# Mixture-of-experts layer on one core: expert rows gathered in 32-column strips and turned by VectorE instead of TensorE

## The chip, the cores and the metric

The kernel runs on one core of a Trainium2 chip. The metric is the device time of one execution in microseconds (us). Three executions of the kernel before took 930.4, 930.9 and 931.77 us; the median is 930.9 us. Engines are called by these names: TensorE (PE in the profile, with its weight loads as PEld), VectorE (DVE), ScalarE (ACT), GpSimd (POOL), SyncE (SP). An engine name with a q (SPq, ACTq) is that engine's instruction queue, from which DMAs are issued.

## The reference

Everything is float32. `x` has 4 batches of 1024 tokens with 512 columns. Each batch picks one of 64 weight matrices by `itok`; after that linear layer the 4096 tokens go to 8 experts, top-1, with at most 512 tokens per expert:

```python
xf   = x @ W[itok] + b[itok]                   # 4096 x 512
prob = softmax(xf @ Wr);  e = argmax(prob)     # 8 experts
keep = rank of the token within its expert < 512
xe   = xf[dispatch]                            # (8, 512, 512): gathered rows
h    = relu(xe @ W1[e])                        # 512 x 2048 per expert
ye   = (h @ W2[e]) * prob of the token         # 512 x 512 per expert
y[dispatch] += ye
out  = x + y
```

## The kernel before, in words

All large products use Strassen-Winograd steps: a product of 2 x 2 blocks is made of seven products numbered k = 1 to 7, and VectorE makes the sums of blocks that they need. Partial results of several k are accumulated in one PSUM bank (`BANK`, L145: k = 1, 4, 6, 7 in bank x; 3, 5 in y; 2 in z), and between two products of one bank a VectorE or ScalarE instruction reads what has been accumulated so far. A product that follows in the same bank has to wait for that read.

**Stage 1 (0 to 147 us): the batch's linear layer and the router.** Chunks of 512 tokens of `x` are loaded (`load_x`, L245, on SP's queue; the first chunk in four pieces), turned by TensorE (`transpose_x`, L265), multiplied (`linear`, L470), and VectorE adds the bias while it empties PSUM (`plus_bias`, L501, and `finish`, L516). `done` (L509) writes each 256-token result to DRAM, in two arrays `xc0_dram` and `xc1_dram`, one for each half of the columns (1 KB per token and array). The router ranks the tokens and scatters, per expert slot, the token's number and probability into `slots` in DRAM (`rank`, L441). `table` (L637) reads them back, and GpSimd makes row indices of them (L642).

**Stage 2 (147 us to the end): the experts, one after the other, about 96 us each.** `fetch(e)` (L698) is called after the second group of the first layer. GpSimd gathers by indirect DMA (`gather`, L682) the residual rows of `x` for expert e, four gathers of 128 rows x 2 KB, and the rows of the next expert e+1 from `xc0_dram` and `xc1_dram`, eight gathers of 128 rows x 1 KB. `transpose_rows` (L707) turns a tile of 128 rows with four TensorE transposes into PSUM; ScalarE copies them to `xe` (VectorE does it for expert 0), and after the last tile VectorE makes four sums of `xe` blocks (L727 to L733). `xe` has a single buffer, so nothing of the next expert can be written before the last first-layer product of this expert has read it.

The first layer is `first_layer` (L740) for four groups g of hidden units, `xe` as the moving side and W1 as the weights. The second layer (`second_layer`, L795) does the products k = 1, 6, 7 whole, and k = 2, 5, 3, 4 by a second Strassen step: `inner_sums` (L815) makes twelve VectorE sums or differences at most per k, and `inner_product(e, k, q)` (L851) the small products q = 1 to 7, written "(k, q)" below. The order at the end of an expert (L952 to L984) is: second layer 1; inner sums 2; second layer 6; inner sums 5; **turn tile 0 of the next expert**; small products (2,1), (2,5), (2,2), (2,6), (2,3), (2,7); **turn tiles 1 and 2**; (2,4); inner sums 3; second layer 7; inner sums 4; (5,5), (5,2); **turn tile 3**; then the rest of (5,q), (3,q), (4,q). Products (2,7) and (2,4) both write bank x. At the last expert no tiles are turned, since there is no next one. GpSimd scatters the finished rows at the end (L889).

**What sets the order.** The program lists the order of TensorE and of SP's queue by hand (`manual_schedule`). For VectorE, ScalarE and GpSimd the order is worked out when the kernel is built, from the program's order as priority and an expected time at which each instruction's inputs are ready; `soon` and `high_priority` move a call up, `behind` ties it to an earlier instruction. On the chip each engine then runs its list strictly in that order: an instruction whose input is not there holds up everything behind it.

Of the kernel before, what the change touches and what calls it, by code (L numbers as in the profile page):

```python
# [16 lines left out]
P = 128  # L17
# [5 lines left out]
def kernel(  # L23
# [29 lines left out]
    W1G = 3  # L53
    NS = E * SC
    Q = 32
    ROW = 2
# [26 lines left out]
    def unordered(group, ins):  # L83
# [12 lines left out]
    nc.vector.memset(wr_sb, 0.0)  # L96
    nc.scalar.dma_start(
        out=wr_sb[:, :, 0:E], in_=wr.rearrange("(kc p) e -> p kc e", p=P)
    )
    zeros = const.tile([P, T * ROW // P], F32, name="zeros")  # L100
    nc.vector.memset(zeros, 0.0)
    slots = dram.tile([T, ROW], F32, name="slots")
    nc.scalar.dma_start(out=slots.rearrange("(p s) r -> p (s r)", p=P), in_=zeros)
    before = const.tile([P, P], F32, name="before")
# [25 lines left out]


    xc_dram = [dram.tile([T, HD], F32, name=f"xc{j}_dram") for j in range(2)]

    table = const.tile([P, SC, E, ROW], F32, name="table")
    src_row = const.tile([P, NS], I32, name="src_row")
    dst_row = const.tile([P, NS], I32, name="dst_row")

# [36 lines left out]
    def load_w1(e, g):  # L174

        t = w1p.tile([P, 7, HK, HB * P], F32, tag="w1", name=f"w1_{e}_{g}")
        for half in range(2):
            f = half * F // 2 + g * HB * P
            nc.sync.dma_start(
                out=t[:, 2 * half : 2 * half + 2, :, :].rearrange("p a k f -> p (a k) f"),  # L180
                in_=w1[e, :, f : f + HB * P].rearrange("(k p) f -> p k f", p=P),
            )
        w1s[e, g] = t

# [4 lines left out]
    with (  # L189
# [54 lines left out]

        def load_x(c):  # L245
            t = xin.tile([P, XT, D], F32, tag="x", name=f"x_{c}")
            n = 1 if c == 0 else XT
            for j in range(0, XT, n):
                nc.sync.dma_start(
                    out=t[:, j : j + n, :],  # L250
                    in_=xf[c * CT + j * P : c * CT + (j + n) * P, :].rearrange(
                        "(j p) d -> p j d", p=P
                    ),
                )
            xrows[c] = t
# [214 lines left out]
        def linear(b, g, k):  # L470
# [15 lines left out]
            for j in range(2):  # L486
                for kc in range(HK):
# [11 lines left out]
                    )  # L499

            def plus_bias(into, half):  # L501
                return nc.vector.tensor_tensor(
                    into,
                    ps,
                    bias[:, half * HD : (half + 1) * HD].unsqueeze(1).to_broadcast([P, 2, HD]),
                    ALU.add,
                )

            def done(t, i, j):  # L509
                at = c * CT + i * HT  # L510
                nc.sync.dma_start(
                    out=xc_dram[j][at : at + HT, :].rearrange("(j p) d -> p j d", p=P),
                    in_=t,
                )

            def finish():  # L516
# [10 lines left out]
                if k in (2, 3):  # L527
                    t = banks.pop((key, 1 if k == 2 else 6))
                    latest[0] = nc.vector.tensor_tensor(t, ps, t, ALU.add)
                    done(t, 0, int(k == 3))  # L530
                if k == (7 if b < B - 1 else 5):
                    t = banks.pop((key, 7))
                    nc.vector.tensor_tensor(t, banks[key, "y"], t, ALU.add)
                    done(t, 1, 1)
                    if b == LATE:
                        t = banks[key, 6]
                        nc.vector.tensor_tensor(t, banks[key, "y"], t, ALU.add)
                if k == 4:
# [82 lines left out]
        with tc.manual_schedule(engines={mybir.EngineType.PE, mybir.EngineType.SP}):  # L621
            load_x(0)
            load_batch(0)
            load_x(1)
            load_batch(1)
            load_x(2)
            load_batch(2)
            keep_warm(ps_t, 3)
            for i in range(XT):
                transpose_x(0, i)  # L630
            for b in range(B):
                for i, product in enumerate(ORDERS[b]):
                    linear(*(b, *product)[-3:])
                    for f, *at in loads.get((b, i), []) + beside.get((b, i), []):
                        f(*at)
# [21 lines left out]

    rows, residual, xes, hs = {}, {}, {}, {}

    def load_w2(e, when=None):  # L660
# [21 lines left out]
    def gather(e, pool, sources, into, at):  # L682

        n = D // len(sources)
        for j, source in enumerate(sources):
            for c in range(SC):
# [9 lines left out]
                )  # L696

    def fetch(e):  # L698

        at = rowp.tile([P, 2 * SC], I32, tag="at", name=f"at_{e}")  # L700
        n = min(2 * SC, NS - e * SC)
        nc.vector.tensor_copy(at[:, 0:n], src_row[:, e * SC : e * SC + n])  # L702
        gather(e, xr, [xf], residual, at[:, 0:SC])
        if e + 1 < E:
            gather(e + 1, xg, xc_dram, rows, at[:, SC : 2 * SC])

    def transpose_rows(e, c, parts=range(2)):  # L707

        if e not in xes:
            xes[e] = xep.tile([P, 7, HK, HC * P], F32, tag="xe", name=f"xe_{e}")  # L710

        t = xes[e]
        r = rows[e * SC + c]
        half, at = divmod(c, HC)
        n = len(parts)
        lo = parts[0] * HK
        ps = ps_e.tile([P, KC, P], F32, tag="t", name=f"ps_e_{e}_{c}_{lo}")
        for kc in range(n * HK):
            nc.tensor.transpose(ps[:, kc, :], r[:, (lo + kc) * P : (lo + kc + 1) * P], ident)
        (nc.vector.tensor_copy if e == 0 else nc.scalar.copy)(  # L720
            t[
                :, 2 * half + parts[0] : 2 * half + parts[0] + n, :, at * P : (at + 1) * P
            ].rearrange("p b k n -> p (b k) n"),
            ps[:, 0 : n * HK, :],
        )
        if c == SC - 1:
            b11, b21, b12, b22, t1, t2, t4 = (t[:, k, :, :] for k in range(7))  # L727
            if 0 in parts:
                nc.vector.tensor_tensor(t1, b12, b11, ALU.subtract)
            if 1 in parts:  # L730
                nc.vector.tensor_tensor(t2, b22, t1, ALU.subtract)
                nc.vector.tensor_tensor(b12, b22, b12, ALU.subtract)
                nc.vector.tensor_tensor(t4, b21, t2, ALU.subtract)  # L733

# [187 lines left out]
    with tc.manual_schedule(engines={mybir.EngineType.PE, mybir.EngineType.SP}):  # L922
        gather(0, xg, xc_dram, rows, src_row)

        for part, half, then in (
            ([0], 0, [(0, 1)]),
            ([0], 1, [(1, 1), (0, 5), (1, 5)]),
            ([1], 0, [(0, 2)]),
            ([1], 1, [(1, 2)]),
        ):  # L930
# [6 lines left out]
        for e in range(E):  # L937
# [25 lines left out]

            def ahead(*tiles):
                for c in tiles:
                    if e + 1 < E:
                        transpose_rows(e + 1, c)

            second_layer(e, 6)
            inner_sums(e, 5)  # L970
            ahead(0)
            small(*[(2, q) for q in (1, 5, 2, 6, 3, 7)])
            ahead(1, 2)
            small((2, 4))
# [3 lines left out]
            small((5, 5), (5, 2))  # L978
            ahead(3)
            small(  # L980
# [37 lines left out]
```

## Time and profile before

| What | Value |
|---|---|
| Median of three runs | 930.9 us |
| The profiled execution | 930.86 us |
| Span of its instructions (first to last) | 929.1 us |
| TensorE busy in the span, matmuls | 915.9 us |
| TensorE transposes of gathered rows (L719) | 128, of which 112 are of experts 1 to 7 |
| VectorE busy | 654.9 us |
| GpSimd busy | 181.7 us |
| Mean DMA rate | 133 GB/s |
| Granted TensorE clock | 0.998 |
| Packets under 512 B | 8516 of 95727 |

The span is 1.8 us shorter than the time of the same execution; that remainder lies around the instructions. A timeline row gives the start and the length of a group of like instructions, then engine, line, operation, output and inputs, sizes and count, and in brackets how long the engine had been idle before it and what ended that. Matmuls overlap, so a row of eight 128 x 128 products that starts every 0.89 us is listed as 1.06 us long; what counts is the distance from one start to the next. The same holds for VectorE, where a sum of 128 x 512 elements is listed as 0.68 us long and starts every 0.60 us.

### The profile page before, as it was taken

What the parts mean: (1) busy time and instruction counts of PE and PEld (TensorE: products, weight loads), DVE (VectorE), ACT (ScalarE), POOL (GpSimd) and SP (SyncE); (2) the same over time, 40 slices, a digit from 0 to 9 for tenths busy, and PEclk for the clock granted to TensorE, in tenths of its full rate; (3) what the DMA queues carried; (4) which work ended last, traced back from release to release, by engine and by line L of the source; (5) the groups of instructions that cost most, each with busy time, mean ns of one, the idle gap of its engine ahead of it and who ended that gap; (6) DMA issues with size and microseconds to landing.
All of it is one profiled execution on the core that took longest, in us unless ns stands there. A gap on an engine that the chain in (4) does not pass through costs nothing.

```text
span 929.1 us, 13272 instructions
## 1 busy us (share of the span) xinstructions
PE 915.9 (99%) x5318; PEld 817.5 (88%) x5318; DVE 654.9 (70%) x1222; ACT 193.5 (21%) x350; POOL 181.7 (20%) x173
## 2 busy tenths in 40 slices
PE   9999999999999999999999999999999999999996
PEld 6788787889988998899889988999889988998886
DVE  4656684589549954987488847883789368945793
ACT  3323200321132103210331023112311132113200
POOL 0043443060141013201230024001500150012001
PEclk9999999999999999999999999999999999999999
DMA  8475223992372118310841085106520562044001
GB/s 299 157 242 167 81 80 117 343 379 90 100 254 100 46 61 266 127 47 21 275 152 46 1 277 164 58 1 227 182 91 2 202 202 90 2 154 159 1 1 46
DMA packets 95727, 123.32 MB, mean 133 GB/s; under 512 B 8516, under 2 KB 83268, under 8 KB 95474
## 3 DMA queue, kind: packets, MB, share of 16 engines
q1 hardware_dynamic: 85634, 97.54, 31.5%
q0 software_dynamic: 9216, 24.85, 8.1%
q8 instruction: 42, 0.69, 0.3%
q10 hardware_dynamic: 816, 0.08, 0.1%
q14 instruction: 19, 0.16, 0.1%
HBM read 105.96 MB, written 25.23 MB: 141 GB/s over the span
## 4 chain that ended last, share of the span: by engine, by line
PE 64%; issue 18%; DVE 13%; POOL 3%; DMA 1%; ACT 0%; POOLq 0%; DVEq 0%
PE hx L746 19%; PE hy L746 9%; PE yx L856 7%; PE xcx_lin L488 6%; PE hz L746 5%; PE yx L803 4%; PE yy L856 3%; DVE rows L791 2%; PE xcy_lin L488 2%; POOL rows L691 2%; DVE h L160 2%; DVE h L161 2%; PE ps_xT L273 1%; PE xcz_lin L488 1%; DVE h L163 1%
## 5 line engine op out<-in xcount | busy, mean ns | idle before, releaser
L746 PE MATMUL hx<-xe,w 128*128 128x256 f32 x1024 | 237.7, 379 | 1.2 <-DVE xe L720 1.0
L746 PEld LDWEIGHTS hx<-xe,w 128*128 128x128 f32 x1024 | 193.8, 190 | 27.7 <-DVE xe L720 1.2
L889 POOL DMA_INDIRECT out_dram<-rows,dst_row x32 | 32.0, 999 | 465.3 <-DVE rows L791 428.6
L746 PE MATMUL hy<-xe,w 128*128 128x256 f32 x512 | 120.6, 379 | 0.0
L803 PE MATMUL yx<-w_b,h 128*128 128x256 f32 x512 | 113.1, 379 | 0.0
L746 PEld LDWEIGHTS hy<-xe,w 128*128 128x128 f32 x512 | 97.3, 190 | 13.2
L803 PEld LDWEIGHTS yx<-w_b,h 128*128 128x128 f32 x512 | 96.7, 190 | 12.8
L761 ACT COPY s<-hx 128x512 f32<-128x512 f32 x96 | 55.8, 582 | 222.7 <-PE hx L746 222.7
L765 DVE TENSOR_TENSOR h<-hy,s 128x512 f32<-128x512 f32 x64 | 44.1, 688 | 76.0 <-PE hy L746 51.7
L766 ACT ACTIVATE h<-h 128x512 f32<-128x512 f32 x96 | 60.5, 630 | 150.7 <-DVE h L765 150.7
L856 PE MATMUL yx<-w_b,h 128*128 128x128 f32 x640 | 83.4, 275 | 0.7 <-DVE rows L791 0.6
L791 DVE SCALAR_TENSOR_TENSOR rows<-yx,table,rows 128x128 f32<-128x128 f32 (+1 forms) x160 | 59.9, 398 | 30.8 <-PE yx L856 30.7
L856 PEld LDWEIGHTS yx<-w_b,h 128*128 128x128 f32 x640 | 77.3, 192 | 1.1 <-DVE rows L791 1.0
L691 POOL DMA_INDIRECT rows<-in_x_dram,at x32 | 45.2, 1412 | 145.4 <-DVE at L702 106.2
L691 POOL DMA_INDIRECT rows<-xc_dram,at x56 | 58.4, 1043 | 21.4 <-issue 14.3
L746 PE MATMUL hz<-xe,w 128*128 128x256 f32 x256 | 60.6, 379 | 0.6 <-DVE xe L720 0.6
L765 DVE TENSOR_TENSOR h<-hz,s 128x512 f32<-128x512 f32 x32 | 22.0, 688 | 55.4 <-PE hz L746 55.4
L803 PE MATMUL yx<-w_t,h 128*128 128x256 f32 x256 | 56.6, 379 | 0.0
L460 POOL DMA_INDIRECT slots<-row,dest x32 | 36.3, 1136 | 96.4 <-DVE dest L456 87.9
L746 PEld LDWEIGHTS hz<-xe,w 128*128 128x128 f32 x256 | 48.5, 190 | 7.4 <-DVE xe L720 0.9
L803 PEld LDWEIGHTS yx<-w_t,h 128*128 128x128 f32 x256 | 48.6, 190 | 6.6
L856 PE MATMUL yx<-w_t,h 128*128 128x128 f32 x384 | 52.1, 279 | 0.4
(160 smaller groups left out, 1244.3 us busy)
## 6 DMA issues: line engine op xcount, KB each, us to landing
w<-in_L_ffn_W_dram SPq DMA_DIRECT2D x64, 512.0 KB, 4.3
w_b<-in_L_ffn_W_dram SPq DMA_DIRECT2D x32, 1024.0 KB, 10.9
x<-in_x_dram SPq DMA_DIRECT2D x7, 1024.0 KB, 8.7
xc_dram<-s SPq DMA_DIRECT2D x22, 256.0 KB, 2.7
out_dram<-in_x_dram SPq DMA_DIRECT2D x2, 2816.0 KB, 20.3
cw<-in_L_cond_W_dram SPq DMA_DIRECT2D x3, 1024.0 KB, 10.6
out_dram<-in_x_dram SPq DMA_DIRECT2D x1, 2560.0 KB, 12.2
xc_dram<-xc SPq DMA_DIRECT2D x8, 256.0 KB, 2.3
```

The costliest lines, as they stand in the source:

```text
L160: eng.tensor_tensor(s1, a21, a22, ALU.add)
L460: nc.gpsimd.indirect_dma_start(out=slots, out_offset=bass.IndirectOffsetOnAxis(ap=dest[:, j : j + 1], axis=0), in_=row[:, j, :], in_offset ...
L488: nc.tensor.matmul(ps[:, j, :], lhsT=left[:, kc, j * P : (j + 1) * P], rhs=right[k][:, kc, :], start=((k in OPENS or (b, k) == (LATE, 3)) ...
L691: nc.gpsimd.indirect_dma_start(out=into[e * SC + c][:, j * n : (j + 1) * n], out_offset=None, in_=source, in_offset=bass.IndirectOffsetOnA ...
L746: nc.tensor.matmul(ps[:, j, :], lhsT=w1s[e, g][:, LEFT[k], kc, j * P : (j + 1) * P], rhs=xes[e][:, RIGHT1[k], kc, :], start=(k in OPENS an ...
L761: nc.scalar.copy(banks[key, k], ps)
L765: latest[0] = nc.vector.tensor_tensor(into, ps, part, ALU.add)
L766: nc.scalar.activation(into, into, AF.Relu)
L791: nc.vector.scalar_tensor_tensor(row, ps, table[:, half * HC + at, e, 0:1], row, ALU.mult, ALU.add)
L803: nc.tensor.matmul(ps[:, at, :], lhsT=hs[e][:, m // HB, LEFT[k], m % HB, at * P : (at + 1) * P], rhs=w2s[e][RIGHT2[k]][:, m, :], start=(k ...
L856: nc.tensor.matmul(ps, lhsT=left[:, g, :], rhs=right[:, g, :], start=(q in OPENS and g == 0), stop=(q == LAST[BANK[q]] and g == NG - 1), s ...
L889: nc.gpsimd.indirect_dma_start(out=of, out_offset=bass.IndirectOffsetOnAxis(ap=dst_row[:, n : n + 1], axis=0), in_=residual.pop(n), in_off ...
```

## The change

For experts 1 to 7 the rows are no longer gathered whole. The column order of `xc0_dram` and `xc1_dram` is permuted, so that the 256 columns of a half lie in four strips of 64. A gather then fetches, for 32 rows, all four strips, each into its own 32 partitions: 128 descriptors of 256 B. An expert needs 32 such gathers in place of 8. In SBUF the tile is then a set of 32 x 32 squares each of which only has to be turned in place, and four VectorE instructions of 128 x 512 elements per expert (`turn_strips`) do so, writing straight to `xe`. Sixteen TensorE transposes and four ScalarE copies per expert go away. Expert 0 keeps the old way; since the columns of its rows are now permuted, its W1 is loaded in a matching order, by 16 DMAs of 64 KB per group in place of 2 of 512 KB. New index tables (`strips`, `src_strip`) are made once, by four DMAs on ScalarE's queue and eight small GpSimd instructions. Apart from that the first chunk of `x` is loaded through ScalarE's queue, ahead of `wr` and the zeros for `slots`, and one of three warming matmul pairs at the start is dropped.

```diff
@@ load_w1
+            into = t[:, 2 * half : 2 * half + 2, :, :]
+            if e > 0:
...
+                continue
+            rows_of = w1[e, :, f : f + HB * P].rearrange(
+                "(a k q b c) f -> b k c a q f", a=2, k=HK, b=2, c=V
+            )
+            for b in range(2):
+                for k in range(HK):
+                    lo = (b * HK + k) * V
+                    for a in range(2):
+                        nc.sync.dma_start(out=into[lo : lo + V, a], in_=rows_of[b, k, :, a])
@@ linear: plus_bias, done, finish
+            def strip(t):
+                return t.rearrange("p j d -> p (j d)").rearrange(
+                    "p (b j k c) -> p j k b c", b=VB, j=2, c=V
+                )
+            def bank_of(t):
+                return t.rearrange("p j (k b c) -> p j k b c", b=VB, c=V)
...
+                return nc.vector.tensor_tensor(strip(into), bank_of(ps), bank_of(added), ALU.add)
...
-                    out=xc_dram[j][at : at + HT, :].rearrange("(j p) d -> p j d", p=P),
-                    in_=t,
+                    out=xc_dram[j][at : at + HT, :].rearrange(
+                        "(j p) (b d) -> p b j d", p=P, b=VB
+                    ),
+                    in_=t.rearrange("p j d -> p (j d)").rearrange(
+                        "p (b j d) -> p b j d", b=VB, j=2
+                    ),
@@ start
-            load_x(0)
+            load_x(0, nc.scalar)
             load_batch(0)
+            nc.scalar.dma_start(
+                out=wr_sb[:, :, 0:E], in_=wr.rearrange("(kc p) e -> p kc e", p=P)
+            )
+            nc.scalar.dma_start(out=slots.rearrange("(p s) r -> p (s r)", p=P), in_=zeros)
...
-            keep_warm(ps_t, 3)
+            keep_warm(ps_t, 2)
@@ new functions
+    def strip_rows():
+        for b in range(VB):
+            nc.scalar.dma_start(
+                out=strips[b * V : (b + 1) * V].rearrange("r a c e w -> r a (c e w)"),
+                in_=slots.rearrange("(a r s) w -> r a (s w)", a=VB, r=V),
+            )
+        into = src_strip.rearrange("p e (c a) -> p e c a", a=VB)
+        for a in range(VB):
+            row = strips[:, a, :, :, 1].rearrange("p c e -> p e c")
+            nc.gpsimd.tensor_scalar(row, row, FAR, float(T - 1), ALU.add, ALU.min)
+            nc.gpsimd.tensor_scalar(
+                into[:, :, :, a], row, float(VB), strip_at, ALU.mult, ALU.add
+            )
+    def gather_strips(e, at):
+        for half in range(2):
+            for j in range(2):
+                t = xg.tile([P, D], F32, tag="rows", name=f"strips_{e}_{half}_{j}")
+                n = D // (HC * VB)
+                for q in range(HC * VB):
+                    c = half * HC * VB + q
+                    nc.gpsimd.indirect_dma_start(
+                        out=t[:, q * n : (q + 1) * n],
+                        out_offset=None,
+                        in_=xc_dram[j].rearrange("t (b d) -> (t b) d", b=VB),
+                        in_offset=bass.IndirectOffsetOnAxis(ap=at[:, c : c + 1], axis=0),
+                    )
+                rows[e, half, j] = t
+    def turn_strips(e, half, j):
+        t = rows.pop((e, half, j)).rearrange("p (q k c) -> p k q c", k=HK, c=V)
+        into = xe_of(e)[:, 2 * half + j, :, :].rearrange("p k (q r) -> p k q r", r=V)
+        nc.vector.transpose(into, t)
@@ order at the end of an expert
             second_layer(e, 6)
             inner_sums(e, 5)
-            ahead(0)
             small(*[(2, q) for q in (1, 5, 2, 6, 3, 7)])
-            ahead(1, 2)
+            if e + 1 < E:
+                for half in range(2):
+                    for j in range(2):
+                        turn_strips(e + 1, half, j)
             small((2, 4))
             inner_sums(e, 3)
             second_layer(e, 7)
             inner_sums(e, 4)
             small((5, 5), (5, 2))
-            ahead(3)
+            if e + 1 < E:
+                sum_xe(e + 1)
```

## The prediction, made before the changed kernel was run

> **What bounds the kernel now.** First the page: which engine is full, and what the transposes cost as a group (line, engine, operation, output and input, sizes, count, busy us and mean ns, idle time before).
>
> ```profile
> PE 915.9 (99%) x5318; PEld 817.5 (88%) x5318; DVE 654.9 (70%) x1222; ACT 193.5 (21%) x350; POOL 181.7 (20%) x173
> ...
> L719 PE MATMUL ps_e<-ident,rows 128*128 128x128 f32 x128 | 18.3, 273 | 0.4 <-DMA rows<-xc_dram,at 0.4
> L720 ACT COPY xe<-ps_e 128x512 f32<-128x512 f32 x28 | 15.7, 588 | 80.2 <-PE ps_e L719 80.2
> ```
>
> (The second and third line are from the groups by form.) TensorE has no gaps worth naming, at a clock of 0.998, so an instruction less on it is the only thing that shortens the run, provided TensorE then doesn't wait. Hence the second view: who is just behind it at the end of an expert. The windows give span, then busy time of PE, PEld, DVE, ACT, POOL:
>
> ```profile
> 333.10:429.30 96.20, 96.15 (x561) 87.62 (x562) 70.87 (x125) 19.85 (x36) 17.43 (x16) 1.00 0.37 121
> ...
> 401.50:425.20 23.70, 23.70 (x162) 22.18 (x160) 23.63 (x46) 2.78 (x6) 0.00 (x0) 1.00 0.12 42
> ```
>
> Over a whole expert VectorE has 25 us free, but in the stage from which the transposes are taken it is as full as TensorE: 23.63 of 23.70 us. The third view is TensorE's timeline there, for expert 2 (with transposes), then for expert 7, which has no next expert and so no transposes:
>
> ```profile
> 411.70 1.06 PE L856 MATMUL yx<-w_b,h 128*128 128x128 f32 x8
> 412.60 1.04 PE L719 MATMUL ps_e<-ident,rows 128*128 128x128 f32 x8
> 413.47 1.06 PE L856 MATMUL yx<-w_b,h 128*128 128x128 f32 x8
> ```
>
> ```profile
> 892.91 1.16 PE L856 MATMUL yx<-w_b,h 128*128 128x128 f32 x8
> 894.63 1.16 PE L856 MATMUL yx<-w_b,h 128*128 128x128 f32 x8 [0.56 <-DVE rows L791]
> ```
>
> The yx rows are (2,7) and (2,4), of one bank. In expert 2 eight transposes fill the 0.87 us between them; in expert 7, without them, TensorE stands until VectorE has read the bank, and (2,4) starts 1.72 us after (2,7) instead of the usual 0.89: a stall of 0.83. Last, GpSimd's gathers at expert 0:
>
> ```profile
> 203.19 1.45 POOL L691 DMA_INDIRECT rows<-xc_dram,at  x1 [0.30 <-issue]
> 204.94 1.08 POOL L691 DMA_INDIRECT rows<-xc_dram,at  x1 [0.30 <-issue]
> 210.65 1.19 POOL L691 DMA_INDIRECT rows<-xc_dram,at  x1 [4.62 <-DMA rows<-in_x_dram,at]
> ```
>
> They come late and behind a DMA backlog (DMA share about 1.0 from 162 to 212 us).
>
> **1. Transposes off TensorE.** Four take 0.44 us from start to start (406.80 to 407.24), so 16 take 1.75, and seven experts 12.3 us. That is the ceiling. But they were also fillers. Expert 7 shows the same list without them: from the end of second layer 6 (888.20) to the last pair (919.51) is 31.31 us; expert 2 takes 406.80 to 439.09, 32.29. So 0.98 us per expert, not 1.75; the rest is the stall at (2,4). Expert 7 also lacks the xe sums on VectorE. Expert 2 has with them waits of about 0.2 us before (5,6) (425.49) and 0.1 before (5,4), which expert 7 lacks; those stay. I take 0.98 - 0.30 = 0.68, seven times: **-4.8 us**. At expert 0 the wait of 0.4 for a gathered tile in mid-transpose goes too: **-0.4**. ScalarE's 28 copies were beside other work: 0.
>
> **2. Four turns per expert on VectorE.** No turn is in the trace. The nearest row is a 128x512 sum, 0.68 us, 0.60 from start to start: four are 2.4 us. Here the Trainium skill speaks against the change ("VectorE: DVE Perf Modes", section "The three transpose paths" and the rules after it): a 128x128 bf16 takes 311 ns on VectorE, in 32x32 squares, and TensorE is advised where PSUM will do. An expert has 16 such blocks, so by the page 5.0 us (an estimate from its bf16 figure). With either, VectorE's list gets longer where it is full. Inner sums 4 end at 425.2; with 2.4 us ahead of them 427.6, with 5.0 us 430.2. TensorE needs them for (4,5) at 431.05, less the 0.7 gained: 430.3. With the row's figure there are 2.7 us to spare, with the page's 0.1. Inner sums 3 (end 418.8, needed by (3,5) at 426.49) have more. So 0, with the row's figure; with the page's the small PSUM reads also come late, 0 to 1 us per expert. A gain is excluded: nothing leaves VectorE's list.
>
> **3. Gathers: 32 for 8.** A gather is 0.95 us plus 0.30 between, for 1 KB rows and other sizes of piece alike (1.14 mean for the 8-byte scatters). So 1.25 x 32 = 40 us where it was 10. In expert 2 they start at 368.38, end at 408.4, and land (median 3.0) at 411.4. The turns stand in the list after inner sums 5, which end at 413.7; the fourth turn starts at 415.5. The GpSimd scatters behind them come only at 437. So 0, with 2 to 4 us of cover; lost cover stops VectorE, one for one. In bytes nothing changes, but packets are 256 B. "DMA: Bandwidth & Descriptors", section "Specifications", puts the line rate at 512 B and above. The software queue's 24.85 MB take 8.1% of 16 engines' 929 us, so an expert's 1.05 MB take some 3.2 us of all 16 engines (an estimate), twice that if halved in rate, beside a DMA share of 0.37: 0. No run here shows such packets.
>
> **4. The same at expert 0.** Gathers start at 198.1; six are out by 206.0, the queue waits until 210.65, eight are out by 213.2, the other 24 take 30 us: 243.2, landed at about 246. Quarters arrive near 216, 226, 236, 246. The old transposes were at 214 to 231. The first product of expert 1 that needs all four quarters is k = 6, at 248.41 + 3.45 - 1.1 = 250.8; turn and sums need some 2 us after 246. So it just fits **if** VectorE's list has the third and fourth turn behind the other work. If they stand at their place in the program (221 us), VectorE stops, and with it the reads that free TensorE's banks. The list isn't in program order: W1 sums run between the earlier-listed h sums at 361 to 365 us, because readiness counts. So an expected late landing puts the turns later. But the expectation can be early: at 12.18 VectorE waits 0.6 us for a bias DMA placed ahead of ready work. Bounds 0 and about 18 us: (3,5) at 234.0 would wait for a turn at 246.2 and then inner sums 3, 8 x 0.60. I take 0, with doubt.
>
> **5. Between the stages.** xc writes have 1024 runs of 256 B for 256 of 1 KB. One issue was 0.36 us; w_b loads of 1024 runs took 1.41 (5.64 for four). So SP is held about 1 us more per write. Only the last writes count: gathers of the second half start at 151.21, rows are needed at 156.29, and with 1.25 per gather and 3.0 to land the second tile arrives at about 155.5. A delay of 1 to 3 us leaves 0 to 2: **+1.0**. The eight index instructions (0.32 to 0.36 each, 2.8 in all) fit GpSimd's 5.4 us gap before 151.21; in front of the gathers they'd cost up to 2.8. W1 of expert 0: 14 more SP issues per group at 0.36, 5 us, in front of xc writes (88.78) and, at 174, of output copies; two buffers per partial result cover it: 0, at most 2. VectorE's evictions into runs of 32: a permuted read (L368, 287 ns) costs what a plain one does (L81, 286): 0; doubled they'd still fit, 91 of 147 us busy plus 38.
>
> **6. The start.** One warming pair less is 2 x 0.855 = 1.71 us; transposes begin right behind it (6.74). The x pieces, issued 1.14 to 2.95, land 3.5 later, 4.6 to 6.5, so not all can be used; from ScalarE's queue they start no later, and weights (3.99) leave SP up to 1 us earlier. ScalarE's first copy is at 7.82, wr needed at 16: hidden. Bounds 0 and -1.71: **-1.0**.
>
> Sum: -4.8 - 0.4 + 1.0 - 1.0 = -5.2. The profiled execution took 930.86 us (span 929.1 plus 1.8 around it), equal to the median 930.9: about 925.5.
>
> **The rivals.**
> - *A full gain*: VectorE's reads come at once, nothing stalls: 930.9 - 12.3 - 1.7 = 917. Against it stands expert 7's (2,4). Chance 0.05.
> - *Expert 0 stops VectorE* (slower): part 4 by the list of turns in program order, or with turns three and four at the expected, too early, times. A stop of 5 to 18 us, likeliest 12: 925.5 + 12 = 937.5. It decides from 5 us on, that is when a turn stands more than 5 us ahead of its landing. For it: the backlog, the in-order list. Against: readiness is weighed, and 2 us of the list are enough slack once it is. Chance 0.28.
> - *VectorE becomes the bound of every expert*: turns at 5.0 us or more, stalls of 0.7 to 1.5 us seven times: 930 to 936. Chance 0.12.
> - *The forecast*: 920 to 929, chance 0.55.
>
> **How the numbers follow.** A measurement of this kernel tells 0.2% (1.9 us) from no change. Faster: 0.52 of the forecast's 0.55 and the full gain's 0.05, so 0.57; same 0.11, from the edges of all; slower 0.32, from the other two. The range 918 to 940 leaves out the full gain and the worst of the stop.
>
> **What would show it.** (2,4) starting about 1.7 us after (2,7) in experts 0 to 6 (right), or 0.9 (full gain). Experts about 95.5 us apart instead of 96.24. Turns near 0.7 us. In the waits, no VectorE wait for gathered rows; if there is one of many us at expert 0, part 4 failed; if one in each expert, part 3. An end of stage 1 later than now beyond 1 us would show part 5 wrong; a first product (9.44) at about 8.4, part 6 right.

## The result, and the profile after

The changed kernel takes 1000.2 us (median of four runs, 999.16 to 1000.93) where the kernel before takes 930.9: 1.074 times as long, interval 1.072 to 1.076. The forecast was 925.5 with a range up to 940. The profiled execution took 999.16 us with a span of 997.4, 68.3 more than the 929.1 of before.

The experiments ran in seven sessions, and five of these (1, 3, 4, 6 and 7) were disturbed: the kernel before took 931.8 to 932.9 us there instead of 930.8, some of the semaphore updates are missing from every trace, and kernels with many small gathers saw some releases 7 us and more late, so that numbers are compared only within a session.

The page of the changed kernel: engines, the gathers, products that TensorE stood in front of, and the turns (busy us, mean ns, idle before).

```profile
PE 924.4 (93%) x5204; PEld 820.7 (82%) x5204; DVE 670.4 (67%) x1257; ACT 177.9 (18%) x322; POOL 366.5 (37%) x353
...
L753 POOL DMA_INDIRECT strips<-xc_dram,at x224 | 242.0, 1080 | 74.1 <-issue 66.1
...
L929 PE MATMUL yx<-w_b,h 128*128 128x128 f32 x640 | 92.5, 294 | 27.8 <-DVE rows L864 27.7
...
L791 DVE STREAM_TRANSPOSE xe<-strips 128x512 f32<-128x512 f32 x28 | 19.1, 699 | 69.9 <-DMA strips<-xc_dram,at 38.2
```

TensorE has 114 instructions less and is busy for longer, 924.4 us for 915.9: part of its work ran at a lower clock. The 28 turns take 0.70 us each, and VectorE stood for 69.9 us in front of them. The waits of the changed kernel say for what (us in total, times, longest):

```profile
DVE xe L791 <- DMA strips<-xc_dram,at: 38.2, 8, 8.6
DVE xe L791 <- issue: 31.7, 7, 7.1
PE yx L929 <- DVE rows L864: 27.7, 16, 5.2
PE yx L876 <- DVE h L163: 24.0, 7, 6.5
```

These are 15 waits, about two for each of the seven experts that are turned so. All are for gathered strips, those named "issue" too: each of the 15 turns starts 0.27 to 0.28 us after the landing of the last gather of its own tile. TensorE's waits are for the VectorE work that is queued behind the turns. In expert 2 VectorE's timeline shows the order of its list:

```profile
428.14 0.69 DVE L838 TENSOR_TENSOR h<-hy,s 128x512 f32<-128x512 f32 x1 [0.61 <-PE hy L819]
428.75 1.29 DVE L791 STREAM_TRANSPOSE xe<-strips 128x512 f32<-128x512 f32 x2
429.97 0.70 DVE L162 TENSOR_TENSOR h<-h 128x512 f32<-128x512 f32 x1
434.96 0.71 DVE L791 STREAM_TRANSPOSE xe<-strips 128x512 f32<-128x512 f32 x1 [4.28 <-DMA strips<-xc_dram,at]
435.60 0.65 DVE L163 TENSOR_TENSOR h<-h 128x512 f32<-128x512 f32 x1
436.16 0.75 DVE L164 TENSOR_TENSOR h<-h 128x512 f32<-128x512 f32 x1
436.84 0.68 DVE L165 TENSOR_TENSOR h<-h 128x512 f32<-128x512 f32 x1
437.44 0.72 DVE L162 TENSOR_TENSOR h<-h 128x512 f32<-128x512 f32 x1
442.74 0.71 DVE L791 STREAM_TRANSPOSE xe<-strips 128x512 f32<-128x512 f32 x1 [4.57 <-issue]
```

The first turns stand right behind the last first-layer sum (L838), and not behind inner sums 5. The third stands among the sums of `h` of the last group (the first L162 to L165), the fourth among those of inner sums 2 (the second L162 on). Both are reached before their strips are there; GpSimd's last gather for this expert is

```profile
439.94 0.94 POOL L753 DMA_INDIRECT strips<-xc_dram,at  x1 [0.30 <-issue]
```

TensorE in the same stretch:

```profile
436.30 1.99 PE L876 MATMUL yx<-w_t,h 128*128 128x256 f32 x8 [3.01 <-DVE h L163]
438.13 1.05 PE L929 MATMUL yx<-w_b,h 128*128 128x128 f32 x8
439.02 1.06 PE L929 MATMUL yy<-w_b,h 128*128 128x128 f32 x8
439.91 1.06 PE L929 MATMUL yz<-w_b,h 128*128 128x128 f32 x8
445.72 2.07 PE L929 MATMUL yx<-w_b,h 128*128 128x128 f32 x8 [4.75 <-DVE rows L864]
447.59 1.92 PE L929 MATMUL yy<-w_b,h 128*128 128x128 f32 x8
449.29 1.91 PE L929 MATMUL yx<-w_b,h 128*128 128x128 f32 x8
451.65 1.27 PE L929 MATMUL yx<-w_b,h 128*128 128x128 f32 x8 [0.44 <-DVE rows L864]
```

Two stops, 3.01 and 4.75 us, and behind the second the products start 1.7 to 1.9 us apart, not 0.89. The windows show why (span, busy time of PE, PEld, DVE, ACT, POOL, then the granted clock):

```profile
370.90:476.68 105.78, 97.57 (x547) 88.47 (x545) 73.22 (x130) 17.59 (x32) 44.14 (x41) 0.97 0.35 110
440.80:445.70 4.90, 0.17 (x2) 0.00 (x0) 2.96 (x7) 0.00 (x0) 0.08 (x1) 0.94 0.04 8
445.70:452.70 7.00, 6.54 (x32) 6.24 (x33) 5.54 (x12) 0.00 (x0) 0.00 (x0) 0.56 0.00 0
452.70:459.70 7.00, 7.00 (x35) 6.17 (x35) 6.84 (x13) 0.00 (x0) 0.00 (x0) 1.00 0.00 0
```

For the 7 us behind the stop the clock is 0.56. Every stop of 4.6 us or more in this trace brings a clock of 0.5, and of the eight stops of 2.4 to 3.6 us half do. Which ones, the trace shows too. Its nine drops of the clock up to the last product all begin on one grid of 3.413 us: the first is at 216.39 us, and the others (243.70, 339.27, 445.09, 550.90, 646.47, 656.71, 752.29 and 854.69) come 8, 36, 67, 98, 126, 129, 157 and 187 times 3.413 us behind it. In the stretch of the grid just before each drop TensorE had, by its matmul rows, been idle for 2.4 us or more; in every other stretch at full clock, for 1.7 us or less. So the stop of 2.69 us before 646.14, which lies within the stretch from 643.06 to 646.47, lowered the clock, and the stop of 3.01 us before 436.30, which a border of the grid at 434.85 splits into 1.56 and 1.45 us, did not. The Trainium skill ("TensorE: Matmul & The Clock Gate", part 1, on the clock gate) says that the array falls to half its rate after an idle window of about 3.4 us that runs freely; this trace agrees on the length of the window, on its free running and on the half rate, but here the window did not have to be idle throughout.

Expert 0, where the gathers came late before too: the first and the last of its turns on VectorE, and TensorE behind the last:

```profile
217.87 0.71 DVE L791 STREAM_TRANSPOSE xe<-strips 128x512 f32<-128x512 f32 x1 [7.13 <-issue]
...
242.43 0.71 DVE L791 STREAM_TRANSPOSE xe<-strips 128x512 f32<-128x512 f32 x1 [8.59 <-DMA strips<-xc_dram,at]
```

```profile
249.74 2.08 PE L929 MATMUL yx<-w_t,h 128*128 128x128 f32 x8 [9.12 <-DVE p L83]
```

Expert 2 in sum: stops 3.01 + 4.75 + 0.44 = 8.2; the four products from 445.72 to 452.76 take 7.04 us for 3.57 at full clock, less the 0.44 already counted, 3.0; less the 1.75 of the transposes: 9.5, and the measured difference is 105.78 - 96.24 = 9.54. Over the run, taken at the start of each expert's last matmul instruction: expert 0 costs 18.6 us (266.91 for 248.29), experts 1 to 6 together 51.2 (628.8 for 577.6), expert 7 nothing (95.26 both times), and what follows the last product is 1.5 shorter: 68.3.

### The profile page after: what moved, and what is told of

The parts are those of the page before. It is cut to its first block, busy times and chain, and to the rows that moved or that the text cites. A ratio compares the mean times of both kernels' runs of the same rounds, so it can differ in the third digit from the quotient of the medians.

```text
span 997.4 us, 13408 instructions
## 1 busy us (share of the span) xinstructions
PE 924.4 (93%) x5204; PEld 820.7 (82%) x5204; DVE 670.4 (67%) x1257; ACT 177.9 (18%) x322; POOL 366.5 (37%) x353
## 4 chain that ended last, share of the span: by engine, by line
PE 43%; POOL 23%; issue 22%; DMA 7%; DVE 4%; POOLq 0%; SPq 0%; DVEq 0%
POOL strips L753 19%; PE yx L929 8%; PE hx L819 7%; PE xcx_lin L502 6%; PE yy L929 4%; DMA strips<-xc_dram,at 4%; PE yx L876 3%; POOL rows L738 3%; PE hy L819 3%; PE hz L819 2%; PE xcy_lin L502 2%; PE yz L929 2%; DMA rows<-in_x_dram,at 1%; PE xcz_lin L502 1%; PE ps_xT L287 1%
## 5 line engine op out<-in xcount | busy, mean ns | idle before, releaser
L753 POOL DMA_INDIRECT strips<-xc_dram,at x224 | 242.0, 1080 | 74.1 <-issue 66.1
L929 PE MATMUL yx<-w_b,h 128*128 128x128 f32 x640 | 92.5, 294 | 27.8 <-DVE rows L864 27.7
L929 PEld LDWEIGHTS yx<-w_b,h 128*128 128x128 f32 x640 | 85.5, 207 | 32.2 <-DVE rows L864 31.3
L876 PEld LDWEIGHTS yx<-w_b,h 128*128 128x128 f32 x512 | 96.7, 190 | 12.8
L838 DVE TENSOR_TENSOR h<-hy,s 128x512 f32<-128x512 f32 x64 | 44.0, 688 | 75.5 <-PE hy L819 50.8
L738 POOL DMA_INDIRECT rows<-in_x_dram,at x32 | 41.5, 1298 | 140.6 <-DVE at L766 91.1
L876 PE MATMUL yx<-w_t,h 128*128 128x256 f32 x256 | 64.5, 410 | 24.0 <-DVE h L163 24.0
L876 PEld LDWEIGHTS yx<-w_t,h 128*128 128x128 f32 x256 | 51.6, 204 | 34.3 <-DVE h L163 26.8
L791 DVE STREAM_TRANSPOSE xe<-strips 128x512 f32<-128x512 f32 x28 | 19.1, 699 | 69.9 <-DMA strips<-xc_dram,at 38.2
L838 DVE TENSOR_TENSOR h<-hz,s 128x512 f32<-128x512 f32 x32 | 22.0, 687 | 55.4 <-PE hz L819 55.4
```

The source lines that it names most:

```text
L738: nc.gpsimd.indirect_dma_start(out=into[e * SC + c][:, j * n : (j + 1) * n], out_offset=None, in_=source, in_offset=bass.IndirectOffsetOnA ...
L753: nc.gpsimd.indirect_dma_start(out=t[:, q * n : (q + 1) * n], out_offset=None, in_=xc_dram[j].rearrange("t (b d) -> (t b) d", b=VB), in_of ...
L838: latest[0] = nc.vector.tensor_tensor(into, ps, part, ALU.add)
L876: nc.tensor.matmul(ps[:, at, :], lhsT=hs[e][:, m // HB, LEFT[k], m % HB, at * P : (at + 1) * P], rhs=w2s[e][RIGHT2[k]][:, m, :], start=(k ...
L929: nc.tensor.matmul(ps, lhsT=left[:, g, :], rhs=right[:, g, :], start=(q in OPENS and g == 0), stop=(q == LAST[BANK[q]] and g == NG - 1), s ...
```

## The experiments

Theory A: the strips land too late for the place that the turns have in VectorE's list; VectorE stops, then TensorE, and then its clock drops. Theory B, the rival: the many small gathers slow down the other engines by themselves, wherever they stand.

**Late turns (session 1).** The turns stand behind `inner_sums(e, 4)` and are tied to its last difference.

```diff
-            if e + 1 < E:
-                for half in range(2):
-                    for j in range(2):
-                        turn_strips(e + 1, half, j)
             small((2, 4))
...
             inner_sums(e, 4)
+            if e + 1 < E:
+                with tc.issue_after(inner["last"].ins):
+                    for half in range(2):
+                        for j in range(2):
+                            turn_strips(e + 1, half, j)
```

> The changed kernel with its four turns tied behind the last difference of inner sums 4 in VectorE's list. Theory (place in the list): VectorE stops because the turns stand about 10 us before their rows land, right where xe is released. Then moved back, VectorE has no wait for strips at experts 1 to 6, these come 95.3 to 96 us apart, and only expert 0 still waits some 10 us, since its rows land at 242: 930 to 938 us in all. Rival (load): the 32 gathers, their small packets or VectorE's extra work themselves hold TensorE back, wherever the turns stand: 985 us or more.

1012.7 us (before: 932.1). No gain, against theory A, but in a disturbed session.

**Turns that wait for no gather (session 1).** The gathers run, and the turns read a tile of zeros, so experts 1 to 7 compute with zeros.

```diff
-        t = rows.pop((e, half, j)).rearrange("p (q k c) -> p k q c", k=HK, c=V)
+        rows.pop((e, half, j))
+        t = idle.rearrange("p (q k c) -> p k q c", k=HK, c=V)
```

> The changed kernel with turns that read a constant tile in place of the gathered strips (so experts 1 to 7 compute with zeros), in the same places of VectorE's list; all gathers still run. Theory (place): without the wait everything else costs nothing, 923 to 928 us: the start gains 1.8, the seam between the stages loses about 1, each expert gains 0.5 to 1. Rival (load): stays above 985. If VectorE's four extra instructions at this place cost TensorE something, expert distances lie above 96.24.

1009.3 us, with single runs from 990 to 1031. No turn waits in its trace, and TensorE still stops for up to 6.0 us at a time. That too spoke for theory B; it was not measured in an undisturbed session.

**Eight gathers (session 1).** Eight gathers of 128 x 1 KB instead of 32 of 128 x 256 B; the same turns at the same place, which then turn other squares than the reference's.

```diff
-                n = D // (HC * VB)
-                for q in range(HC * VB):
+                n = HD
+                for q in range(HC):
...
-                        in_=xc_dram[j].rearrange("t (b d) -> (t b) d", b=VB),
+                        in_=xc_dram[j],
```

> The changed kernel with eight gathers of 128 pieces of 1 KB per expert in place of 32 of 256 B (whole rows, so the squares turned aren't those of the reference); the turns wait for them as before. Theory (place and gather count): the rows land 30 us earlier, experts 1 to 6 have no wait, expert 0 at most 5 us: 924 to 931 us. Rival (turns): if the turns as such are what costs, it stays above 985.

921.1 us, 0.988 of before (0.986 to 0.989), with experts 1 to 6 94.83 to 95.48 us apart. Everything of the change is in this kernel except the number and size of the gathers. Turns, evictions in strips, permuted writes and W1 loads therefore cost less than the transposes gave; the loss comes with the 32 gathers. (2,7) and (2,4) in expert 2 of this kernel:

```profile
407.69 1.06 PE L929 MATMUL yx<-w_b,h 128*128 128x128 f32 x8
409.19 1.16 PE L929 MATMUL yx<-w_b,h 128*128 128x128 f32 x8 [0.45 <-DVE rows L864]
410.19 7.07 PE L876 MATMUL yx<-w_b,h 128*128 128x256 f32 x32
```

1.50 us apart, a stall of 0.61.

**Warming in the stop (session 1).** Two warming pairs behind (2,2) in experts 0 to 6, to see what of the loss is the clock.

```diff
-            small(*[(2, q) for q in (1, 5, 2, 6, 3, 7)])
+            small(*[(2, q) for q in (1, 5, 2)])
+            if e + 1 < E:
+                keep_warm(ps_e, 2)
+            small(*[(2, q) for q in (6, 3, 7)])
```

> The changed kernel with two idle 128x512 products (3.4 us) on TensorE behind (2,2), where it stands for 3.6 to 5.2 us per expert. Theory (clock): the products behind the stop run at half speed because the granted clock falls when TensorE stands; busy through the stop, it stays at 1.0, and the run is 10 to 20 us shorter than the changed kernel: 980 to 990 us. Rival: the slow products have another cause (VectorE's reads of PSUM, the weights), and it stays at 1000 or goes up by what the idle products take.

1050.2 us (single runs from 1028.8): neither.

**The changed kernel again (session 2).** No edit.

> The changed kernel itself once more, as the measure for the others on this chip. In the first four experiments the turns moved behind inner sums 4, and turns that wait for no gather, gave 1013 and 1009 us, so that the wait of the turns can't be all. Both theories expect 1000 us here (as first measured); a value of 1010 or more says that the four were measured where the changed kernel itself is slower.

1003.1 us (before: 930.8), experts 1 to 6 105.65 to 106.02 apart, no updates missing from the trace: the measure for the next three.

**Early gathers (session 2).** From expert 1 on the strip gathers are issued one group earlier, ahead of the residual gathers. VectorE's list keeps its turns.

```diff
+        if g == 0 and e > 0:
+            behind(fetch_strips, e)
         if g == 1:
             behind(fetch, e)
```

> From expert 1 on, the 32 strip gathers stand at the expert's first group, ahead of the residual gathers: some 25 us earlier; the turns stay where they are. Theory A (the gathers end too late: the turn stands in VectorE's list ahead of the landing, TensorE stops, and its clock drops behind the stop): experts 1 to 6 lose their 7.7 to 9.5 us, so 1000 - 6 x 9 = 946 us, experts about 95.5 apart. Theory B (while many small gathers run, the other engines get their releases late, wherever the gathers stand): 985 us or more, with waits in the first layer in place of those at the turns.

954.2 us, 1.024 of before (1.023 to 1.026); 49 us of the 72 are gone. VectorE in expert 2:

```profile
423.23 0.68 DVE L842 TENSOR_TENSOR h<-hy,s 128x512 f32<-128x512 f32 x1
423.83 1.29 DVE L795 STREAM_TRANSPOSE xe<-strips 128x512 f32<-128x512 f32 x2
425.05 0.65 DVE L162 TENSOR_TENSOR h<-h 128x512 f32<-128x512 f32 x1
425.62 0.70 DVE L795 STREAM_TRANSPOSE xe<-strips 128x512 f32<-128x512 f32 x1
...
428.62 0.70 DVE L795 STREAM_TRANSPOSE xe<-strips 128x512 f32<-128x512 f32 x1
```

The order up to the fourth turn is that of the changed kernel (its sum L838 is L842 here), but the last gather is done at 414.7 us, 14 us before that turn. No bracket stands at a turn, and TensorE's clock is 1.0 from 257 us to the end of the last expert. The 32 gathers are all still there. Of the 23 us that remain, expert 0 has 20.1. That the gathers cost something by themselves wherever they stand is false for an undisturbed session. That they cost something only beside the small products is left to the next experiment.

**More gathers in the kernel before (session 2).** 24 more gathers of 128 x 256 B per fetch into a tile that nobody reads.

```diff
             gather(e + 1, xg, xc_dram, rows, at[:, SC : 2 * SC])
+            for i in range(24):
+                nc.gpsimd.indirect_dma_start(
+                    out=spare[:, i % 6 * 64 : (i % 6 + 1) * 64],
...
```

> The kernel before with 24 more gathers of 128 x 256 B per fetch (7 fetches, 168 in all), into a tile that nobody reads, behind the 8 that it needs; nothing waits for them but later GpSimd work. Theory A: no wait is added, 931 to 934 us (GpSimd is done at 408 of the scatters' 437 us in expert 2). Theory B: the load alone costs what it costs in the changed kernel, 980 us or more.

929.6 us, 0.999 of before (0.998 to 0.999). 168 gathers and 190.6 us of GpSimd time cost nothing if nobody waits for them:

```profile
379.37 0.95 POOL L708 DMA_INDIRECT spare<-xc_dram,at  x1 [0.30 <-issue]
...
412.61 1.41 POOL L708 DMA_INDIRECT spare<-xc_dram,at  x1 [0.30 <-issue]
...
L708 POOL DMA_INDIRECT spare<-xc_dram,at x168 | 190.6, 1135 | 51.2 <-issue 50.3 <-DMA spare<-xc_dram,at 0.6 <-DVE rows L799 0.3
```

In expert 2 they run until 414.0 us, 71 us behind the expert's start, beside the small products; in the changed kernel the strips run until 70 us behind it. Late gathers without a waiting turn cost nothing, and early gathers with the turns in place take the waits away: together this shows theory A for experts 1 to 6 in an undisturbed session.

**First two experts whole (session 2).** As early gathers, and expert 1 handled like expert 0 (gathered whole, turned by TensorE, its W1 in the permuted order).

```diff
-            if e > 0:
+            if e > 1:
...
+            if e == 0:
+                turn_rows(1, 0)
```

> As the one with early gathers, and expert 1 as well gathered whole and turned by TensorE like expert 0 (its W1 in the permuted order too), so that no strip gather falls into the DMA backlog of expert 0. Theory A: 930.9 - 1.9 (start, as measured in the first profile) + 1.1 (seam) - 6 x 0.7 to 1.4 = 922 to 926 us. Theory B: 980 us or more.

946.8 us, 1.017 of before (1.015 to 1.018); the expected 922 to 926 were missed. Expert 0's last matmul is back at 248.78 us (248.29 before), so the 18.6 us lost there were the strips of expert 1. But expert 1 took 105.84 us, with a TensorE stop of 5.4, and the others 97.1. Its waits between 248 and 356 us:

```profile
DVE rows L883 <- DMA rows<-in_x_dram,at: 7.5, 2, 4.9
```

These are residual rows, which now stand behind 32 strip gathers on GpSimd: a wait that the edit itself made.

**Residual gathers first (sessions 3, 4 and 5).** The same, with the four residual gathers ahead of the strips.

```diff
         gather(e, xr, [xf], residual, at[:, 0:SC])
         if e == 0:
             gather(1, xg, xc_dram, rows, src_row[:, SC : 2 * SC])
+        else:
+            fetch_strips(e)
...
-        if g == 0 and 0 < e < E - 1:
-            behind(fetch_strips, e)
-        if g == 1:
+        if g == (e == 0):
```

> As the one with experts 0 and 1 whole and early strip gathers, but with the four residual gathers ahead of the 32 strip gathers. In that one VectorE waited 1.3 to 1.7 us per expert (4.9 at expert 1) for residual rows, and experts lay 97.1 us apart. Theory A: without that wait experts 2 to 6 lie 95 to 95.5 apart and expert 1 near 96: 930.8 - 1.9 (start) + 1.1 (seam) - 6 x 0.9 = 925 us, 922 to 928. If the 97.1 us come from the many gathers themselves, 944 to 948 us stay.

1121.7 us in session 3, a disturbed one. Again:

> Residual gathers ahead of the early strip gathers, once more, for the same reason (1122 us in the last session). Theory A: 922 to 928 us, experts 2 to 6 95 to 95.5 us apart. If 940 us or more stay with no update missing, 36 gathers in a row early in the expert cost something that 32 did not.

1126.0 us in session 4, also disturbed. In session 3 ScalarE waited for products (L855) that TensorE's own rows show as done: the 16 `hx` of TensorE run from 403.53 to 407.25, and

```profile
402.89 0.59 ACT L855 COPY s<-hx 128x512 f32<-128x512 f32 x1 [2.08 <-remote]
414.91 0.59 ACT L855 COPY s<-hx 128x512 f32<-128x512 f32 x1 [11.43 <-remote]
```

By itself in a session:

> Residual gathers first, by itself in a session. If the session, and not the kernel, made the 1122 and 1126 us (updates missing in the traces of every kernel of these sessions): 922 to 928 us by theory A, with no update missing. If it takes 1100 us again, and the trace of this kernel alone lacks updates too, then 36 gathers in a row at an expert's start are what brings the late releases about.

930.6 us, 1.000 of before (1.000 to 1.001), no updates missing. One program takes 930.6 and 1122 us, so the late releases come with the session. Experts 2 to 6 are 94.83 to 94.96 apart (one 96.32), as in the kernel with eight gathers, so the 97.1 of early gathers were late residual rows. The gain of 5.6 us in experts 2 to 6 doesn't reach the time: in the profiled execution expert 1 costs 2.8 us more than before (98.99 for 96.23; TensorE waits 1.5 and 1.3 us in its first layer), and from the last product to the end of the span it is 10.7 us, not 7.9. That the 64 KB pieces of expert 1's W1 make the first and what makes the second is not shown.

**Late turns again (sessions 3, 4 and 6).**

> The same kernel as the first one with late turns (turns behind inner sums 4), measured again, since early gathers removed the waits and 24 idle gathers cost nothing, which the late turns' 1013 us contradict. By theory A (a turn that stands ahead of its landing is what stops VectorE) the late turns too should bring experts 1 to 6 back to 95 to 97 us: 935 to 955 us, with expert 0 still late. If it is 1000 us or more again, the place in the list is not what counts, and the early gathers helped in another way (fewer gathers beside the small products).

1016.9 us.

> Late turns once more. In the two sessions in which it ran, the kernel before took 932.1 and 932.9 us and part of the semaphore updates is missing from the traces; in the session of the early gathers it took 930.8 and none is missing. If releases that come late there (up to 11 us behind the instruction) made the 1013 and 1017 us, then in a session with 930 to 931 us for the kernel before theory A's 935 to 955 us appear. If it is 1000 us or more here too, the place of the turns is not what counts.

1004.1 us.

> The late turns, by themselves in a session; residual gathers first, which took 1122 and 1126 us in two sessions, took 930.6 so. By theory A (the turn's place ahead of the landing): 935 to 955 us, no update missing, no releases that come late, expert 0 still late. If it is 1000 us or more with no update missing, the place doesn't count. If it is 1000 us or more with updates missing, the session is of the disturbed kind again and the place stays unsettled.

1002.1 us by itself. Updates are missing from all three traces, so this is the third of the outcomes foreseen. The later place does take the waits away: in each of the four traces of late turns all turns together wait for 0.8 us, for 69.9 in the changed kernel. But TensorE still stops, in one of them for 24.4 us in the first layer, where no turn stands, and how much of these stops an undisturbed session would leave was not measured. Whether later turns alone would save the change stays open.

**Warming again (sessions 3, 4 and 7).**

> The same kernel as the first one with two warming pairs behind (2,2) in experts 0 to 6, measured again. If the drop of the clock needs a stop of over 3 us in one piece, and the pair cuts the stop of 4.8 us into 1.7 busy and 3.1 idle, the clock stays at 1.0 and 2.9 us per expert are saved: 980 to 985. If the idle time is only moved, or the pair comes when there is no wait: 1000 to 1015.

1040.5 us.

> Two warming pairs behind (2,2), once more, for the same reason. If the clock drops only behind a stop of over 3 us in one piece and the pair cuts the stop: 980 to 985 us, clock near 1.0 in experts 1 to 6. If the idle time is only moved: 1000 to 1015.

1043.6 us.

> Two warming pairs behind (2,2) in experts 0 to 6, by itself in a session. If the clock drops only behind a stop of over 3 us in one piece and the pair cuts the stop of 4.8 us: 980 to 985 us, clock near 1.0 in experts 1 to 6. If the idle time is only moved, or two stops follow each other: 1000 to 1015 us.

1060.3 us. All with updates missing, so the experiment says nothing of an undisturbed session. Against the "over 3 us in one piece" of its theory stands the stop of 2.69 us in the changed kernel, behind which the clock fell. The share of the clock, 3 of 9.5 us in expert 2, is read from the windows and not shown by an experiment.

**The start alone (session 3).** The kernel before with the first chunk of x on ScalarE's queue, `wr` and zeros behind it, and two warming pairs.

> The kernel before with the start of the changed one alone: first chunk of x through ScalarE's queue, wr and zeros behind it, two warming pairs. By the profile after (first product at 7.50 for 9.44) 1.9 us less, 928.9; by the forecast 1.0 less, 929.8. If a later load eats it up, 930.8.

932.0 us to 932.9 of before in that session, 0.9990 (0.9983 to 0.9996): 0.9 us less, near the forecast's 1.0 and below the 0.2% that the prediction counts as told from no change.

No version that computes the reference's output beats the kernel before by more than 0.2%.

## Why the prediction was wrong, point by point

- **Part 3 failed**: "The turns stand in the list after inner sums 5, which end at 413.7 ... So 0, with 2 to 4 us of cover". That place was 70.9 us behind the expert's start (342.85, the last product of expert 1). In the changed kernel the first turn comes 57.9 us behind it (428.75 - 370.90): a turn may run as soon as `xe` is free, that is behind the last first-layer product, and the planner put it there. That is 13 us less cover. Part 4 had said that the list isn't in program order, because readiness counts; part 3 took the place in the program all the same. What landing time the planner reckoned with is not on record. The other term was sized a little short: 44.2 us for 32 gathers (1.08 + 0.30 each) and not 40, so the last strips are there 71.8 us behind the start and not 68.5. In experts 1 to 6 the first two turns were in time, the third and fourth were not. The prediction named the price, "lost cover stops VectorE, one for one", but put no case on it in every expert: its VectorE rival had stalls of 0.7 to 1.5 us. Measured: 7.7 to 9.5 us per expert. Its own sign for this failure, a VectorE wait for gathered rows in each expert, is there. Early gathers with the list kept, and more gathers in the kernel before, show that it was the landing against the place. The 256 B packets, which it put at 0, cost nothing where no turn waits.
- **Part 4 failed** in the direction that it doubted. It took 0, "with doubt", of 0 to 18. Expert 0 costs 18.6 us in all, 19.3 from the seam (161.16 us, 0.7 ahead of before) on: TensorE stops of 6.47 and 9.12 us, each with a clock of 0.53 around it. The strips landed about as reckoned or earlier (217.6, 224.0, 232.8 and 242.2 us, for 216, 226, 236 and 246), but VectorE reached the first turn 7.1 and the fourth 8.6 us before it could start: the place in the list failed, not the landing. The rival "Expert 0 stops VectorE" had this mechanism and 12 us.
- **What neither had**: the clock. A stop was priced at its length; in expert 2 it cost 3.0 us more.
- **Part 1 was right in kind and too small.** Where the gathers are out of the way most experts gain 1.41 us (96.24 to 94.83), not 0.68; with eight gathers two of six took 95.5. The stall at (2,4) is 0.61 and not 0.83, and the waits at (5,6) and (5,4), which were said to stay, are gone. The -0.4 at expert 0 can't be told apart.
- **Part 2 was right**: 0.70 us per turn for the row's 0.68, where the estimate from the Trainium skill ("VectorE: DVE Perf Modes", the three transpose paths) gave 1.24 (four times its figure for a quarter of the elements). In the kernel with residual gathers first the turns wait 2.1 us in the whole run, and TensorE waits for no inner sum.
- **Part 5 was right, and part 6 too small.** The first product starts 1.94 us earlier (7.50 for 9.44), where part 6 took 1.0 with a bound of 1.71. Stage 2 begins at 147.01 for 148.84. Behind its last transposes only 0.7 of these 1.8 us is left (the `hx` row at 161.16 for 161.85), since TensorE waits 0.89 us there for a gathered tile: the seam cost 1.1, where part 5 took 1.0 for a late tile. At the end of the run the start alone is worth 0.9.

## What to carry to other kernels

An in-order engine makes a planner's choice of place part of the cost: when a new instruction depends on a transfer, take the earliest place at which its other inputs allow it, and not its place in the program, and check the landing against that. Making the transfer early is what helped here; a late place was not shown to. Look also at what is queued behind the transfer on the engine that issues it. A stop of TensorE of 4 to 5 us cost more than its length here, since the clock was lower for the 3 to 7 us behind it.

## What was not expected of the hardware

A gather of 128 x 256 B holds GpSimd as long as one of 1 KB (0.94 us for most and 0.30 between them; 1.08 on average, for 1.04 with 1 KB); 32 of them in a row disturb no other engine in an undisturbed session. TensorE's clock went by the idle time in stretches of a grid of 3.41 us, so that a stop of 3 us lowered it or not by where it fell; in the three other undisturbed traces with such stops (the changed kernel again, early gathers, first two experts whole) it dropped behind 2.5 us or more and stayed with 1.7 or less. In a disturbed session the program with the residual gathers first takes 1122 to 1126 us for 930.6, while the kernel before, with 8 gathers in their place, loses 1 to 2 us. What makes a session so is not settled: it isn't the chip, since one chip had sessions of both kinds, and not the kernel.
